# Weights loaded by row chunk, a list schedule with a lower rate for the first loads, and group 1's x transposed on TensorE

## The chip, the cores and the metric

The kernel runs on one core of one Trainium2 chip. The metric is the device time of that core in microseconds (us), the median of several executions. TensorE is called PE in the profile (PEld is its weight load), VectorE is DVE, ScalarE is ACT, GpSimd is POOL, and SP is the engine that issues the DMAs.

## What is computed

Four graph layers run over a batch of 128 graphs with 128 nodes and 512 features each. Every layer adds its result to x and normalizes:

```python
def _layernorm(x, axis=-1, eps=1e-5): ...
# layer 0
Ah = A + eye; dh = rsqrt(sum(Ah, -1)); An = dh[:, :, None] * Ah * dh[:, None, :]
x = _layernorm(x + relu(einsum('bnm,bmf,fc->bnc', An, x, kernel) + bias))
# layer 1
q, k = split(einsum('bnd,ed->bne', x, W_qk)); v = einsum('bnd,ed->bne', x, W_v)
w = softmax(sum((q @ k^T) / 8 * adj, -1), over the nodes)
x = _layernorm(x + w * v)
# layer 2
agg = einsum('bij,bjf->bif', adj, x) / maximum(deg, eps)
x = _layernorm(x + relu(einsum('bnf,of->bno', concat([x, agg]), W)))
# layer 3
L = A_hat * d[:, :, None] * d[:, None, :]            # A_hat = adj + eye
x = _layernorm(x + L @ (x @ W + b))
```

All data are float32. x is 32 MB and adj 8 MB; each of the five 512 x 512 weights (w0, wv, the two halves w2x and w2a of layer 2, and w3) is 1 MB.

## The kernel before

The batch is worked through in 32 groups of G = 4 graphs. A group's x is one tile of 128 partitions (the nodes) by 4 graphs by 512 features, its adjacency one of 128 by 4 by 128. An aggregation is a set of 128x128 matmuls that leave its result transposed (`aggregate`, into PSUM tiles p_agg, copied by ScalarE to agg). A product with a weight (`project`) is done in seven block products in place of eight: for each pair of graphs of a group, the left operand is cut into four blocks (two graphs by two feature halves), the weight into four 256 x 256 blocks, and sums of blocks are multiplied. The names of the seven are B11, T1, B21, B22, T2, T3 and T4. `weight_sums` makes T1 to T4 of a weight by four subtractions on 128x512 elements, `left_sums` the four sums of the left side (agg0s, xT1s, xT2s, agg2s, agg3s in the profile). The products go into PSUM regions named p_o (layers 0, 2 and 3) and p_v (layer 1); VectorE takes them out in steps (u_o, u_v, s_o). The product T4 and what follows it is put off as a "tail", which the next `project` runs after its own B11 (`finish_tails`). `hooks` put other work of TensorE after a named product.

Layer 1 needs x transposed, and there are two ways to do it. `turn_x` writes x to a scratch tensor in DRAM, reads it back in another order (2 + 4 DMAs per half group, xT1s and xT1y) and has VectorE transpose 32 x 32 blocks. `turn_on_tensor` copies x on ScalarE into a tile y, transposes it by 4 matmuls per graph (p_xT) and copies the result back on ScalarE (xT). `l1_turn(t, turn, rows)` takes either.

`begin` (line 829) writes out the order of the first two groups by hand, the loop behind it that of the other 30, and the last lines (879 to 886) that of the last group, in which layers 2 and 3 run for a half group at a time.

The order of the instructions on TensorE is the program's. For all other engines it is set by `Plan.schedule` (line 195), a list schedule made while the kernel is built: `estimate` gives every operation a duration, each gets the latest time at which it must end for TensorE not to wait, and every engine takes of its ready operations the one that is due first. Once issued, each engine works strictly in this order. For DMAs, issued by SP alone, the schedule holds a model of the transfers: the line

```python
bus = max(bus, op.end + self.LAND) + op.size / self.BUS
```

says that they pass one behind another at BUS = 95 elements of 4 bytes per ns, and that the first byte takes LAND = 1600 ns. It also models that a VectorE operation with two operands in SBUF and a GpSimd operation exclude each other (`port`).

At the start the loads of group 0 and 1 go out, then the weights. `weight` loads each by its four blocks, so that a row of a piece is 256 elements (1 KB); wv and w2x come in a permuted row order (`turned`), with 16 DMAs each, the others with 4. The tile is `[P, 7, 2, H]`: block, chunk of 128 rows, column. Behind them come adj and x of groups 2 and 3. adj of group 2 is wanted by `prep_rows(2)`, which sums it (deg), takes the power -1/2 on GpSimd (d), and makes the scaled matrices ana.

All operations are issued from one helper, so nearly all rows of the profile have line 266 and are told apart by their tiles.

Of the kernel before, what the change touches and what calls it, by code (L numbers as in the profile page):

```python
# [10 lines left out]
FP = mybir.dt.float32  # L11
AF = mybir.ActivationFunctionType
ALU = mybir.AluOpType
AX = mybir.AxisListType

P = 128
K = 32
Q = P // K
# [3 lines left out]
H = F // 2  # L22
# [103 lines left out]
class Plan:  # L126
# [4 lines left out]

    ENGINES = ("tensor", "vector", "scalar", "gpsimd", "sync")
    HOP = 200
    LAND, BUS = 1600, 95

    def __init__(self, nc, est):
        self.nc, self.est, self.ops, self.tags, self.group, self.dram = nc, est, [], {}, None, None
# [57 lines left out]
    def schedule(self):  # L195
        number = {op: i for i, op in enumerate(self.ops)}
        for (_, tag, bufs), tiles in self.tags.items():
            used = []
            for t in sorted((t for t in tiles if t.ops), key=lambda t: number[t.ops[0]]):
                if len(used) == bufs:  # L200
                    old = used.pop(min(range(bufs), key=lambda i: number[used[i].ops[-1]]))
                    assert number[old.ops[-1]] < number[t.ops[0]], (tag, bufs)
                    for op in t.ops:
                        if op.preds.isdisjoint(t.ops):
                            op.preds.update(old.ops)
                used.append(t)
        now = 0
        for op in self.ops:
            assert all(number[p] < number[op] for p in op.preds)
            for p in op.preds:  # L210
                p.succs.append(op)
            if op.engine == "tensor":
                op.last = now
                now += op.dur
        for op in reversed(self.ops):
            due = min([s.last - self.hop(op, s) for s in op.succs], default=now)
            op.last = min(op.last, due - op.dur)
        queue = {e: [] for e in self.ENGINES}
        waiting = {op: len(op.preds) for op in self.ops}
        free, bus, port = dict.fromkeys(self.ENGINES, 0), 0, 0  # L220
        pe = [op for op in self.ops if op.engine == "tensor"]
        for op in self.ops:
            if not op.preds:
                queue[op.engine].append((0, number[op], op))
        done = []
        while len(done) < len(self.ops):
            best = None
            for e in self.ENGINES:
                q = queue[e]
                if e == "tensor":  # L230
                    q = [c for c in q if c[2] is pe[0]]
                if not q:
                    continue
                q = [(max(c[0], port if c[2].port else 0),) + c[1:] for c in q]
                at = max(free[e], min(c[0] for c in q))
                pick = min((c for c in q if c[0] <= at), key=lambda c: (c[2].last, c[1]))
                for c in q:
                    if at < c[0] < at + pick[2].dur and c[2].last < at + pick[2].dur and c[2].last < pick[2].last:
                        pick, at = c, c[0]
                if best is None or at < best[0]:  # L240
                    best = at, e, pick[2]
            at, e, op = best
            queue[e] = [c for c in queue[e] if c[2] is not op]
            op.start, op.end = at, at + op.dur
            free[e] = op.end
            if op.port:
                port = op.end
            if e == "sync":
                bus = max(bus, op.end + self.LAND) + op.size / self.BUS
                op.lat = max(op.lat, bus - op.end)  # L250
            if e == "tensor":
                pe.pop(0)
            done.append(op)
            for s in op.succs:
                waiting[s] -= 1
                if not waiting[s]:
                    queue[s.engine].append((max(p.end + self.hop(p, s) for p in s.preds), number[s], s))
        return done
# [48 lines left out]
def kernel(  # L307
# [16 lines left out]
    last = NT - 1  # L324
# [31 lines left out]
    def weight(src, name, queue, turned=False):  # L356


        w = const.tile([P, 7, 2, H], FP, tag=name, name=name)
        for h in range(2):  # L360
            for j in range(2):
                s = src[:, j * H:(j + 1) * H]
                if turned:
                    s = s.rearrange("(b h c k) m -> h b k c m", b=Q, h=2, c=2)[h]
                    for b in range(Q):
                        queue.dma_start(w[b * K:(b + 1) * K, 2 * h + j], s[b])
                else:
                    queue.dma_start(w[:, 2 * h + j], s.rearrange("(h c p) m -> h p c m", h=2, c=2)[h])
        return w

    def weight_sums(w, eng):
        eng.tensor_tensor(w[:, T3], w[:, B22], w[:, T1], ALU.subtract)
        eng.tensor_tensor(w[:, T1], w[:, T1], w[:, B11], ALU.subtract)
        eng.tensor_tensor(w[:, T2], w[:, B22], w[:, T1], ALU.subtract)
        eng.tensor_tensor(w[:, T4], w[:, B21], w[:, T2], ALU.subtract)

    def broadcast_row(src, name, queue):
        r = const.tile([P, F], FP, tag=name, name=name)
# [136 lines left out]
    def project(name, t, parts, first, c11, fin, hooks=None, after=lambda: None, early=True,  # L515
                when=lambda f: f(), pairs=(0, 1)):

        hooks = hooks or {}  # L520
        qs = slice(pairs[0], pairs[-1] + 1)

        def region():
            return ps_b.tile([P, 2, H], FP, tag="pb", name=f"p_{name}_{t}")[:, qs]

        def operand(left_, k):
            s = st[left_, t]
            if isinstance(s, Ref):
                return s.rearrange("p (q r) (h c) n -> p q r h c n", r=2, h=2)[:, :, 0, (B11, B21).index(k)]
            return s[k]  # L530

        def product(p, k, fresh):
            with nc.unit():
                for q in pairs:
                    for i, (left_, w) in enumerate(parts):
                        for c in range(2):
                            nc.tensor.matmul(p[:, q - pairs[0], :], operand(left_, k)[:, q, c, :], w[:, k, c, :],
                                             start=(fresh and q == pairs[0] and i == 0 and c == 0),
                                             stop=(i == len(parts) - 1 and c == 1), skip_group_check=True)
            for f in hooks.get(k, ()):  # L540
                f()

        def block(tag):
            return tp.tile([P, 2, H], FP, tag=tag, name=f"{tag}_{name}_{t}", bufs=1 if tag in ("u5", "sb") else 2)[:, qs]

        g, q, v = region(), None, None
        product(g, B11, True)
        sa, sb = first(g, block)
        finish_tails()
        if early:  # L550
            product(g, B21, False)
            when(lambda: c11(g, block))
        q = region()
        product(q, T1, True)
        u5 = block("u5")
        nc.vector.tensor_tensor(u5, q, sb, ALU.add)
        if not early:
            product(g, B21, False)
            when(lambda: c11(g, block))
        v = region()  # L560
        product(v, T2, True)
        u2 = block("u2")
        nc.vector.tensor_tensor(u2, v, sb, ALU.add)
        product(q, B22, False)
        nc.vector.tensor_tensor(u2, q, u2, ALU.add)
        when(lambda: (fin(0, 1, u2), norm_stats(name, t, 0, pairs)))
        product(v, T3, False)
        nc.vector.tensor_tensor(u5, v, u5, ALU.add)
        fin(1, 1, u5)

        def tail():
            product(v, T4, False)
            nc.vector.tensor_tensor(sa, v, sa, ALU.add)
            fin(1, 0, sa)
            norm_stats(name, t, 1, pairs)
            after()

        tails.append(tail)
# [56 lines left out]
    def l0_agg(t, eng=nc.gpsimd, pairs=(slice(0, 2),)):  # L635
        left("agg0", t)
        for g in range(G):
            aggregate("agg0", t, g, st["anT", t])
        left_sums("agg0", t, eng, pairs)
# [189 lines left out]
    def begin():  # L829
# [3 lines left out]
        weight_sums(w0_sb, nc.gpsimd)  # L833
        l0_agg(0, nc.vector, ONE_BY_ONE)
        prep_rows(1)
        l0_out(0, {B11: [lambda: prep_transpose(1)], B22: [lambda: l0_agg(1)]})
        weight_sums(wv_sb, nc.vector)
        l0_out(1)
        l1_turn(0, turn_on_tensor, (0,))
# [3 lines left out]
        l1_qk(0, 1)  # L843
        for w in (w2x_sb, w2a_sb, w3_sb):
            weight_sums(w, nc.gpsimd)
        l1_turn(1)
        l1_out(0, {B11: [lambda: l1_scores(0)], B21: [lambda: l1_softmax(0)], T3: []})
        finish_tails()
        for r in range(2):
            l1_qk(1, r)  # L850
        l2_both(0, 0)

    def prep(t):
# [23 lines left out]
            l2_agg(t, 0)  # L877

    l2_both(last, 0)
    for q in range(2):  # L880
        l2_out(last, {B21: [lambda: l2_both(last, 1)]} if q == 0 else {}, (q,))
    for q in range(2):
        l3_agg_pair(last, q, nc.gpsimd)
        l3_bias(last, (2 * q, 2 * q + 1))
# [34 lines left out]
```

## Time and profile before

| | |
|---|---|
| runs (us) | 2486.29, 2488.41, 2488.83; median 2488.41 |
| span of the profiled execution | 2486.8 us, mean granted clock 0.997 |
| DMA, core queue | 398624 packets, 240.98 MB, 36.2% of 16 engines |
| SP, first 50 us | 8 loads of adj, x; 44 of the five weights; 4 of W_qk; 2 of biases |
| PE busy, 236 to 312 us (one group) | 76.00 of 76.00 us |
| PE busy, 0 to 100 us | 82.2 of 100 us |
| PE busy, last 27 us | 16.9 of 27 us |

The page's second part cuts the span into 40 slices; its row for PE is 8, then nines, then 8 again, so a group in the middle keeps TensorE busy throughout, and the times at which it is idle lie in the first and last few groups. A chain of waits at these places is read from the timeline: each row has the start, the time spent, engine, operation, tiles, and in brackets the idle time before it with what ended it. The column after the busy times in a table of stretches is the clock that TensorE was granted.

### The profile page before, as it was taken

The numbers are of one execution on the slowest core, as the hardware profiler recorded it, in microseconds if no ns is written. First come the engines' busy times: TensorE is split into PE (matmuls) and PEld (weight loads), VectorE is DVE, ScalarE is ACT, GpSimd is POOL, SyncE is SP. The second block draws the span as 40 slices with busy tenths as digits, with TensorE's granted clock in tenths as the row PEclk, the third lists the DMA queues.
The fourth block names the chain that finished last, engine by engine and source line by source line (L and its number), as shares of the span: only waits on it lengthen the run. The fifth ranks groups of instructions, "written<-read, shape, count | busy, mean of one in ns | idle before, by whom it ended". The sixth has DMA issues, their size and how long they took to land.

```text
span 2486.8 us, 37083 instructions
## 1 busy us (share of the span) xinstructions
PE 2457.3 (99%) x13470; PEld 2206.9 (89%) x13470; DVE 1810.0 (73%) x3169; ACT 973.2 (39%) x1981; POOL 1334.0 (54%) x1522
## 2 busy tenths in 40 slices
PE   8899999999999999999999999999999999999998
PEld 7789988989999899899899998998898999989987
DVE  6677777777777777777777777777777777777665
ACT  2334434343344343343433443433434434443335
POOL 5446555555556464555555564645555555645443
PEclk9999999999999999999999999999999999999999
DMA  5333434333344324343243443343442434423220
GB/s 178 69 93 81 108 88 123 111 78 101 98 106 123 94 77 109 91 124 110 72 107 93 112 123 88 79 111 93 123 110 68 112 90 115 118 81 86 77 60 34
DMA packets 398805, 243.34 MB, mean 98 GB/s; under 512 B 140832, under 2 KB 365600, under 8 KB 398624
## 3 DMA queue, kind: packets, MB, share of 16 engines
q1 hardware_dynamic: 398624, 240.98, 36.2%
q8 instruction: 107, 1.75, 0.3%
q14 instruction: 74, 0.61, 0.1%
HBM read 127.66 MB, written 113.25 MB: 97 GB/s over the span
## 4 chain that ended last, share of the span: by engine, by line
PE 97%; SPq 1%; DVE 1%; DMA 1%; ACT 0%; issue 0%; POOL 0%; ACTq 0%; POOLq 0%; DVEq 0%
PE p_o L266 61%; PE p_v L266 16%; PE p_agg L266 14%; PE p_qk L266 5%; PE p_sc L266 1%; SPq L266 1%; DMA x<-in_x_dram 0%; DVE x L266 0%; PE p_ws L266 0%; ACT xT L266 0%; PE p_w L266 0%; DMA adj<-in_adj_dram 0%; PE p_xT L266 0%; ACT agg L266 0%; DVE wv_sb L266 0%
## 5 line engine op out<-in xcount | busy, mean ns | idle before, releaser
L266 ACT COPY agg<-p_agg 128x512 f32<-128x512 f32 x384 | 221.3, 584 | 573.1 <-PE p_agg L266 573.1
L266 PE MATMUL p_o<-w_sb,agg 128*128 128x256 f32 x1536 | 353.4, 379 | 0.5 <-DVE u_o L266 0.5
L266 PEld LDWEIGHTS p_o<-w_sb,agg 128*128 128x128 f32 x1536 | 286.7, 190 | 37.3 <-DVE u_o L266 0.9
L266 PE MATMUL p_o<-w2x_sb,xT2s 128*128 128x256 f32 x1024 | 263.0, 379 | 3.1 <-DVE xT2s L266 3.1
L266 PE MATMUL p_o<-w2a_sb,agg2s 128*128 128x256 f32 x1024 | 262.8, 379 | 0.0
L266 POOL TENSOR_TENSOR xT1s<-xT 128x512 f32<-128x512 f32 x64 | 94.1, 1471 | 290.2 <-DVE xT L266 220.1
L266 PE MATMUL p_agg<-anT,x 128*128 128x128 f32 x2048 | 243.9, 277 | 0.3 <-DVE anT L266 0.3
L266 PE MATMUL p_o<-w_sb,agg0s 128*128 128x256 f32 x1024 | 230.0, 383 | 7.0 <-DVE u_o L266 5.9
L266 PEld LDWEIGHTS p_agg<-anT,x 128*128 128x128 f32 x2048 | 235.4, 192 | 1.3 <-DVE anT L266 0.6
L266 PE MATMUL p_v<-wv_sb,xT1s 128*128 128x256 f32 x1024 | 233.3, 381 | 0.0
L266 POOL TENSOR_TENSOR agg3s<-agg 128x512 f32<-128x512 f32 x62 | 84.1, 1357 | 272.3 <-ACT agg L266 272.3
L266 PEld LDWEIGHTS p_o<-w_sb,agg0s 128*128 128x128 f32 x1024 | 193.5, 192 | 34.2 <-POOL mro L266 4.9
L266 PEld LDWEIGHTS p_o<-w2x_sb,xT2s 128*128 128x128 f32 x1024 | 194.4, 190 | 29.9 <-DVE xT2s L266 3.6
L266 PE MATMUL p_o<-w_sb,agg3s 128*128 128x256 f32 x992 | 219.2, 379 | 0.0
L266 PEld LDWEIGHTS p_o<-w2a_sb,agg2s 128*128 128x128 f32 x1024 | 194.6, 190 | 26.5
L266 PEld LDWEIGHTS p_v<-wv_sb,xT1s 128*128 128x128 f32 x1024 | 189.6, 190 | 27.3
L266 PEld LDWEIGHTS p_o<-w_sb,agg3s 128*128 128x128 f32 x992 | 188.5, 190 | 25.6
L266 ACT ACTIVATE x<-x,nmro,rstdo 128x512 f32<-128x512 f32 x257 | 198.7, 809 | 4.8 <-ACT nmro L266 0.3
L266 PE MATMUL p_o<-w2x_sb,xT 128*128 128x256 f32 x768 | 197.5, 380 | 1.2 <-ACT s_o L266 0.7
L266 PE MATMUL p_o<-w2a_sb,agg 128*128 128x256 f32 x768 | 197.1, 379 | 0.0
L266 DVE TENSOR_TENSOR u_o<-p_o,s_o 128x512 f32<-128x512 f32 (+1 forms) x132 | 89.2, 675 | 145.3 <-PE p_o L266 145.3
L266 PE MATMUL p_v<-wv_sb,xT 128*128 128x256 f32 x768 | 181.6, 379 | 0.9 <-DVE u_v L266 0.9
(141 smaller groups left out, 4662.1 us busy)
## 6 DMA issues: line engine op xcount, KB each, us to landing
x<-in_x_dram SPq DMA_DIRECT2D x31, 1024.0 KB, 5.1
xT1s<-x SPq DMA_DIRECT2D x124, 256.0 KB, 2.5
xT1y<-xT1s SPq DMA_DIRECT2D x248, 128.0 KB, 3.3
out_dram<-x SPq DMA_DIRECT2D x31, 1024.0 KB, 5.4
xT2s<-x SPq DMA_DIRECT2D x120, 256.0 KB, 2.6
xT2y<-xT2s SPq DMA_DIRECT2D x240, 128.0 KB, 2.8
sa<-ana SPq DMA_DIRECT2D x120, 128.0 KB, 3.3
ya<-sa SPq DMA_DIRECT2D x120, 128.0 KB, 3.2
```

What stands on the lines that cost most here:

```text
L266: getattr(getattr(self.nc, op.engine), method)(*[v.real() if isinstance(v, Ref) else v for v in args], **{k: v.real() if isinstance(v, Ref ...
```

## The change

The weights get tiles `[P, 2, 7, H]`: chunk first, then block. A load brings both column blocks of a row half at once, so that a row of a piece is 512 elements (2 KB). The plain weights take 2 DMAs and the turned ones 8; the sums and the products address the tile by chunk.

The schedule's transfer model takes 62 elements per ns for DMAs issued up to 40 us of the plan and 95 after that, and lets an issue of SP wait until no more than nine DMAs are on their way (this for the whole plan).

In `begin`, the transposes of group 1's adjacency come after the product B21 of group 0's layer 0 instead of after B11. Group 1's x for layer 1 is transposed by `turn_on_tensor`, after the product T3 of group 0's layer 1 (behind the transpose p_ws of its softmax weights), followed by the first half of its p_qk; before, it was turned by `turn_x` ahead of that layer, and both halves of p_qk came after the tail. At the end, the tail of group 30's layer 3 is taken out of the list before layer 2 of the last group, and runs after `l2_both(last, 1)` rather than ahead of it.

```diff
-    LAND, BUS = 1600, 95
+    LAND, FLIGHT = 1600, 9
+    HEAD, BUS = 40000, (62, 95)
...
+            if e == "sync" and len(landed) >= self.FLIGHT:
+                at = max(at, landed[-self.FLIGHT])
             op.start, op.end = at, at + op.dur
...
-                bus = max(bus, op.end + self.LAND) + op.size / self.BUS
+                bus = max(bus, op.end + self.LAND) + op.size / self.BUS[at > self.HEAD]
                 op.lat = max(op.lat, bus - op.end)
+                landed.append(op.end + op.lat)
...
-        w = const.tile([P, 7, 2, H], FP, tag=name, name=name)
+        w = const.tile([P, 2, 7, H], FP, tag=name, name=name)
         for h in range(2):
-            for j in range(2):
-                s = src[:, j * H:(j + 1) * H]
-                if turned:
-                    s = s.rearrange("(b h c k) m -> h b k c m", b=Q, h=2, c=2)[h]
-                    for b in range(Q):
-                        queue.dma_start(w[b * K:(b + 1) * K, 2 * h + j], s[b])
-                else:
-                    queue.dma_start(w[:, 2 * h + j], s.rearrange("(h c p) m -> h p c m", h=2, c=2)[h])
+            to = w[:, :, 2 * h:2 * h + 2].rearrange("p c j m -> p c (j m)")
+            if turned:
+                for b in range(Q):
+                    queue.dma_start(to[b * K:(b + 1) * K], src.rearrange("(b h c k) m -> h b k c m", b=Q, h=2, c=2)[h][b])
+            else:
+                queue.dma_start(to, src.rearrange("(h c p) m -> h p c m", h=2, c=2)[h])
...
-        eng.tensor_tensor(w[:, T3], w[:, B22], w[:, T1], ALU.subtract)
+        eng.tensor_tensor(w[:, :, T3], w[:, :, B22], w[:, :, T1], ALU.subtract)
...
-                            nc.tensor.matmul(p[:, q - pairs[0], :], operand(left_, k)[:, q, c, :], w[:, k, c, :],
+                            nc.tensor.matmul(p[:, q - pairs[0], :], operand(left_, k)[:, q, c, :], w[:, c, k, :],
...
-        l0_out(0, {B11: [lambda: prep_transpose(1)], B22: [lambda: l0_agg(1)]})
+        l0_out(0, {B21: [lambda: prep_transpose(1)], B22: [lambda: l0_agg(1)]})
...
-        l1_turn(1)
-        l1_out(0, {B11: [lambda: l1_scores(0)], B21: [lambda: l1_softmax(0)], T3: []})
+        l1_out(0, {B11: [lambda: l1_scores(0)], B21: [lambda: l1_softmax(0)],
+                   T3: [lambda: l1_turn(1, turn_on_tensor), lambda: l1_qk(1, 0)]})
         finish_tails()
-        for r in range(2):
-            l1_qk(1, r)
+        l1_qk(1, 1)
         l2_both(0, 0)
...
     l2_both(last, 0)
+    held = tails.pop()
     for q in range(2):
-        l2_out(last, {B21: [lambda: l2_both(last, 1)]} if q == 0 else {}, (q,))
+        l2_out(last, {B21: [lambda: l2_both(last, 1), held]} if q == 0 else {}, (q,))
```

## The prediction

> **What bounds the kernel now.** I read the page first, then the waits of TensorE by stage, then its timeline and that of the engine it waits for, and last the stretches with their granted clock.
>
> ```profile
> span 2486.8 us, 37083 instructions
> PE 2457.3 (99%) x13470; PEld 2206.9 (89%) x13470; DVE 1810.0 (73%) x3169; ACT 973.2 (39%) x1981; POOL 1334.0 (54%) x1522
> ```
>
> TensorE is busy for all but 2486.8 - 2457.3 = 29.5 us. The waits of TensorE between 160 and 2380 us are an empty list, so a change of order and of loads can gain only at the two ends. The waits of TensorE from 0 to 160 us (total, times, longest), of which I show the ones that the change touches:
>
> ```profile
> PE p_o L266 <- DVE u_o L266: 5.9, 2, 4.5
> PE p_qk L266 <- DVE xT L266: 3.9, 1, 3.9
> PE p_a L266 <- DVE ana L266: 1.6, 1, 1.6
> ...
> PE p_o L266 <- POOL agg0s L266: 1.0, 1, 1.0
> PE p_v L266 <- DVE u_v L266: 0.9, 1, 0.9
> ```
>
> The timeline of TensorE puts the two long ones at 40.84 to 45.37 us and at 73.77 to 77.66 us. Their price is more than their length, as two stretches show (PE busy, PEld, DVE, ACT, POOL, then the granted clock):
>
> ```profile
> 45.40:51.70 6.30, 6.30 (x18) 5.07 (x19) 2.50 (x6) 2.58 (x5) 5.41 (x7) 0.58 0.04 14
> 77.70:83.10 5.40, 5.40 (x34) 5.40 (x35) 5.40 (x7) 2.75 (x5) 5.13 (x6) 0.68 0.01 3
> ```
>
> Behind each long wait the clock is 0.58 and 0.68. 16 matmuls of 128x256 take 6.32 us there and 3.46 us (16 at 0.2165) in the long rows elsewhere, 2.86 us more; the 32 of p_qk take 5.44 us instead of 2 x 1.78, 1.88 us more. Why the first wait is there, VectorE's timeline says:
>
> ```profile
> 30.93 0.69 DVE L266 TENSOR_TENSOR u_o<-p_o,u_o 128x512 f32<-128x512 f32 x1 [1.87 <-PE p_o L266]
> 35.92 0.69 DVE L266 TENSOR_REDUCE deg<-adj 128x4 f32<-128x512 f32 x1 [4.29 <-DMA adj<-in_adj_dram]
> ...
> 44.55 0.68 DVE L266 TENSOR_TENSOR u_o<-p_o,sb_o 128x512 f32<-128x512 f32 x1
> ```
>
> VectorE stands 4.29 us for adj_2, with the eviction u_o for which TensorE will wait queued behind. adj_2 is issued by SP only at 33.02 us. Between 16.5 and 33 us the DMA moves 2.85 MB at 172 GB/s, against 322 GB/s from 6 to 16 us: there the queue is short of issues. 33 pieces, mostly 64 KB, leave SP at 0.43 us each plus 0.04.
>
> At the end (2380 us on), the page's chain is TensorE until 2438, with one wait inside that the change touches:
>
> ```profile
> PE p_o L266 <- DVE xT2s L266: 1.6, 1, 1.6
> ```
>
> **What the Trainium skill says.** "TensorE: Matmul & The Clock Gate", What's actually happening: an idle window of about 3.4 us puts the array back to half rate, until it has been busy as long. The trace agrees: the 4.53 and 3.88 us waits are followed by 0.58 and 0.68, those of 1.6 us and less by 1.00. "SBUF — State Buffer", Who interferes with whom: a VectorE operation with two inputs in SBUF and a GpSimd operation that reads SBUF exclude each other for a whole instruction. Here the wv_sb subtraction takes 0.69 to 1.76 us, the long ones while GpSimd is busy. "DMA: Bandwidth & Descriptors", Specifications: rows from 512 B on reach line rate. The weights' rows have 1 KB before and 2 KB after, so longer rows alone should give little; the 322 GB/s stretch, mostly packets under 2 KB, agrees.
>
> **The change, part by part.**
>
> Larger pieces. w0, w2a and w3 go from 4 DMAs to 2, wv and w2x from 16 to 8: 22 issues fewer on SP, at 0.47 us some 10 us. In the starved stretch 33 become about 17, 8 us instead of 16.5; the same 2.85 MB at 322 GB/s take 8.9 us. So adj_2 lands about 7.5 us earlier, near 28.5 us instead of 35.9. GpSimd's w2a sum, which stood 11.31 us for its load until 32.11, comes earlier too and no longer sits late before agg0s. The first product needs a 512 KB piece where 256 KB served; all of w0 has landed by 11.43 us before (GpSimd starts its sum then) and the product starts at 12.14: no cost. The strided operands of the 20 subtractions keep 128x512 elements: 0, as the strided xT1s take 1.27 us like the weights.
>
> The plan. Its rate for issues up to 40 us falls from 380 to 248 GB/s (62 elements of 4 B per ns), with at most nine loads in flight. In the plan adj and weights land later than before, so VectorE and GpSimd put other work ahead. Two consequences: d of group 1 (1.01 us on GpSimd, at 12.65 behind the first w0 sum) can go first, at about 10 us, and deg of group 2 leaves its place ahead of u_o. Nine in flight holds for the whole plan; later landings make it careful, not the chip slower.
>
> B11 to B21. The product B21 (8 x 0.2165 = 1.73 us) runs where TensorE stood 1.56 us for ana, and the transposes follow. But VectorE, 13.70 to 25.63 without a pause and stretched by GpSimd, then sets T1, T2 and B22 (waits of 0.16 and 1.34). With d earlier it starts its run about 1.6 us sooner. I take 1.6; bounds 0 (the later waits take it all) and 3.1 (all three go).
>
> The wait for agg0s (1.01): GpSimd starts agg0s at 35.77 behind w2x, although agg is complete at 29.79. With the load early I take 1.0; bounds 0 and 1.0.
>
> The wait for u_o. Without the 4.29 us stand, and with the run before it about 1.6 earlier, VectorE reaches u_o near 44.55 - 4.29 - 1.6 = 38.7; TensorE comes to it at 40.84 - 1.6 - 1.0 = 38.2. Eviction 0.7 and start add up to a wait of about 1.0 in place of 4.53, too short for the slow clock: 3.5 + 2.86 = 6.4. Bounds 1.5 (3 us of wait with a slow clock) and 7.4.
>
> Group 1's x on TensorE. Out go 12 DMAs (2.71 + 4.22 us on SP) and 4 stream transposes (2.49 us of VectorE), and with them the wait of 3.88, its slow clock of 1.88, and the 0.85 for u_v, under which the transposes now lie: 6.6. In come 16 transposes on TensorE (8 take 0.89): 1.8; 4 copies of 0.56 and 4 of 0.59 on ScalarE, which is idle from 66.6 to 78.2 (11.64 us), behind which nothing on the path queues. New: TensorE reaches p_agg of group 0 about 7.3 us after p_ws instead of 12.2. x needs 0.2 for ws, 0.7 for u_v, 1.9 for 4 updates, 1.6 for statistics, 1.3 on GpSimd, 1.0 on ScalarE, 6.8 in all; GpSimd holds two updates up by 2.0 now, and its four xT1s sums may do so. I take a wait of 1.0, net 6.6 - 1.8 - 1.0 = 3.8; bounds 1.5 and 4.8.
>
> The held tail. The 8 matmuls of the last T4 of group 30 (1.73) move from before l2_both(last, 1) into the wait of 1.58 behind it. VectorE's two operations on it (0.69 each) have nothing on the path behind them if they follow xT2s; ScalarE's norm of that group moves some us later, under the products up to 2458. I take 1.4; bounds 0 and 1.6.
>
> Sum: 1.6 + 1.0 + 6.4 + 3.8 + 1.4 = 14.2 us. The profiled execution took 2488.74 by the clock of the other runs, its span being 2486.8; the three runs shown have 2486.29 to 2488.83. 2488.41 - 14.2 = 2474.2. The bounds sum to 3.0 and 17.9.
>
> **Rivals.** (1) VectorE and GpSimd bound the start. From 10 to 50 us they are busy for 28.4 and 24.5 us, and they exclude each other. Then each wait taken out returns at the next eviction, and about half is left: 7, 2481.4. For it: 1.34 follows 1.56 so closely. Against it: 4.29 and 11.31 us of their idle time are waits for loads. (2) The change does little at the start: loads land as before, because bandwidth bounds them, or the plan keeps its order. Then group 1's turn and the tail give 3.8 + 1.4, less what shifts: about 4, 2484.4. Against it: 172 GB/s. (3) Slower: in the steady groups the new plan puts a VectorE operation that waits for a load ahead of an eviction. At 1219.04 a stream transpose stands 0.48 us for its DMA already, at 1246.68 2.16, and B22 starts at 1224.64, only 0.8 us after the T1 eviction ends. Some 29 groups repeat it: 14.2 / 29 = 0.5 us each eats the gain, beyond 0.7 it is slower by more than 0.2%; at 1 us, 2474.2 + 29 = 2503. Against it: SP is idle most of a group, so nine in flight seldom binds, and it makes landings later in the plan, not earlier.
>
> **How the numbers follow.** Forecast 0.72, rival 1 0.13, rival 2 0.08, rival 3 0.07. A measurement of this kernel tells about 0.2%, 5 us, from no change, which ends at 2483.4. Faster: the forecast, rival 1, and 0.03 of rival 2 = 0.88; within: 0.05 of rival 2; slower: rival 3. The range runs from 2470 (the upper bounds nearly all) to 2482.5 (rival 1 with a us to spare), leaving rivals 2 and 3 out.
>
> **What would show it.** In the changed profile: no wait of TensorE over 2 us in the first 100 us, no clock under 0.9 from 10 us on but at the very end; adj_2 landing before 30 us; deg without a wait on DMA ahead of u_o; p_qk of group 1 behind p_xT at once; no xT2s wait at the end; and still an empty list from 160 to 2380 us. A wait list there, a p_agg wait over 3 us at 68 us, or a long wait in the 30s would make it wrong.

## The result and the profile after

The changed kernel takes 2480.97 us (median of 6 runs, 2479.61 to 2481.86) against 2487.88 for the kernel before in the same comparison: 6.9 us less, ratio 0.9972, 95% interval [0.9959, 0.9984]. It is faster, by about half of the 14.2 us that were forecast. The page's head:

```profile
span 2479.5 us, 37052 instructions
PE 2458.4 (99%) x13486; PEld 2206.8 (89%) x13486; DVE 1813.6 (73%) x3165; ACT 976.6 (39%) x1989; POOL 1336.5 (54%) x1522
```

The span is 7.3 us shorter, and TensorE's busy time has hardly moved. The waits of TensorE from 0 to 160 us, as before (total, times, longest):

```profile
PE p_o L270 <- DVE u_o L270: 2.6, 1, 2.6
PE p_v L270 <- DVE u_v L270: 1.9, 1, 1.9
PE p_o L270 <- DVE xT2s L270: 1.5, 1, 1.5
PE p_o L270 <- ACT s_o L270: 1.3, 2, 0.7
...
PE p_o L270 <- DVE agg0s L270: 0.8, 3, 0.4
```

The waits of 4.53 us (u_o), 3.88 (xT), 1.56 (ana) and 1.01 (agg0s) are gone. Two have grown in their place: a wait for u_o of 2.61, which was 1.34, and one for u_v of 1.95, which was 0.85. Their places on TensorE's timeline, and how long the instructions behind them took:

```profile
23.60 1.99 PE L266 MATMUL p_o<-w_sb,agg0s 128*128 128x256 f32 x8 [1.34 <-DVE u_o L266]
...
71.78 1.99 PE L266 MATMUL p_v<-wv_sb,xT 128*128 128x256 f32 x8 [0.85 <-DVE u_v L266]
```

So it was before. In the changed kernel:

```profile
25.10 3.64 PE L270 MATMUL p_o<-w_sb,agg0s 128*128 128x256 f32 x8 [2.61 <-DVE u_o L270]
...
39.06 7.35 PE L270 MATMUL p_o<-w_sb,agg0s 128*128 128x256 f32 x32
...
71.41 2.42 PE L270 MATMUL p_v<-wv_sb,xT 128*128 128x256 f32 x8 [1.95 <-DVE u_v L270]
73.62 3.21 PE L270 MATMUL p_qk<-wqk_sb,xT 128*128 128x128 f32 x16
```

The first product behind the wait of 2.61 takes 3.64 us, where before it took 1.99; behind 1.95, 16 of p_qk take 3.21 where 1.95 to 2.04 is usual. The 32 matmuls at 39.06 run through: there the kernel before stood 4.53 us. The stretches show the slow clock (the column after POOL):

```profile
20.00:30.00 10.00, 7.13 (x29) 5.61 (x30) 7.43 (x13) 0.33 (x1) 2.18 (x2) 0.83 1.05 275
70.00:80.00 10.00, 8.21 (x48) 7.50 (x48) 7.57 (x16) 5.00 (x12) 7.04 (x10) 0.83 0.01 3
```

What VectorE does ahead of both evictions, its timeline says:

```profile
23.10 0.75 DVE L270 TENSOR_TENSOR agg0s<-agg 128x256 f32<-128x256 f32 x2
23.76 0.68 DVE L270 SCALAR_TENSOR_TENSOR x<-u_o,x 128x512 f32<-128x512 f32 x1
24.37 1.28 DVE L270 TENSOR_TENSOR u_o<-p_o,sb_o 128x512 f32<-128x512 f32 x2
...
37.05 0.67 DVE L270 TENSOR_REDUCE deg<-adj 128x4 f32<-128x512 f32 x1
...
66.69 2.68 DVE L270 SCALAR_TENSOR_TENSOR x<-u_v,ws,x 128x256 f32<-128x256 f32 x2
69.29 1.27 DVE L270 BATCH_NORM_STATS2 bnv<-x 128x6 f32<-128x512 f32 x2
...
70.69 0.66 DVE L270 TENSOR_TENSOR u_v<-p_v,u_v 128x512 f32<-128x512 f32 x1
```

VectorE is not idle ahead of u_o at 24.37 or u_v at 70.69. It does work for which nothing on TensorE is waiting: two sums for T3 and an update of x; then updates of x and statistics. The sum of adj_2 (deg, 37.05) no longer waits for its load. From 160 to 2380 us the list of TensorE's waits is still empty.

With TensorE's milestones the 7.3 us fall into the prediction's terms (start of the operation, us). The steps are those of one profiled execution of each kernel; the spans of the changed kernel's six executions lie between 2477.8 and 2480.1 us.

| milestone | before | after | step gains | predicted |
|---|---|---|---|---|
| l0_agg of group 1 (B11 to B21) | 25.43 | 28.58 | -3.15 | +1.6 |
| T1 of group 1 (agg0s) | 37.09 | 39.06 | +1.18 | +1.0 |
| p_ws (the u_o wait) | 70.71 | 65.44 | +7.24 | +6.4 |
| first p_agg of layer 2 (group 1's x) | 82.94 | 76.67 | +1.00 | +3.8 |
| l0_agg of group 2 | 112.25 | 106.21 | -0.23 | 0 |
| the end (held tail), spans | 2486.8 | 2479.5 | +1.26 | +1.4 |

### The profile page after: what moved, and what is told of

Same layout as the page of the kernel before. It is cut to its first block, busy times and chain, and to the rows that moved or that the text cites. A ratio compares the mean times of both kernels' runs of the same rounds, so it can differ in the third digit from the quotient of the medians.

```text
span 2479.5 us, 37052 instructions
## 1 busy us (share of the span) xinstructions
PE 2458.4 (99%) x13486; PEld 2206.8 (89%) x13486; DVE 1813.6 (73%) x3165; ACT 976.6 (39%) x1989; POOL 1336.5 (54%) x1522
## 3 DMA queue, kind: packets, MB, share of 16 engines
q8 instruction: 107, 1.75, 0.3%
## 4 chain that ended last, share of the span: by engine, by line
PE 98%; DMA 1%; ACT 0%; DVE 0%; SPq 0%; POOL 0%; issue 0%; ACTq 0%; POOLq 0%; DVEq 0%
PE p_o L270 62%; PE p_v L270 16%; PE p_agg L270 14%; PE p_qk L270 5%; PE p_sc L270 1%; DMA x<-in_x_dram 0%; SPq L270 0%; DVE x L270 0%; PE p_ws L270 0%; DMA w2x_sb<-in_L_gnn_W_dram 0%; PE p_w L270 0%; ACT xT L270 0%; PE p_xT L270 0%; POOL last L270 0%; ACT agg L270 0%
```

## The experiments

Times are medians, each with the kernel before on the same chip; spans are those of the profiled executions. "Ratio" is to the kernel before.

**e1, the change without the new plan.**

```diff
-    LAND, FLIGHT = 1600, 9
-    HEAD, BUS = 40000, (62, 95)
+    LAND, BUS = 1600, 95
```

> The changed kernel with the schedule's transfer model of before (95 elements per ns throughout, no limit in flight); pieces, order and tail stay. Theory: the lower rate makes VectorE do the last left sums and an x update before the eviction u_o that B22 of group 0 waits for, so without it B22 starts by 23.6 us instead of 25.1 and its clock stays full; the time falls by about 3, to 2478. Rival: the plan is what keeps the sum of adj_2 out of VectorE's way; without it the wait of 4.5 us ahead of group 1's B22 comes back, and the time rises by 3 to 6, to 2484 or more.

Measured: 2491.15 against 2488.06, ratio 1.0012 [1.0006, 1.0019], span 2489.2. The other parts without the plan are slower than no change. The theory held as far as B22 of group 0, which starts at 22.66 us with its clock full. Then the rival's wait comes back: the load of adj_2 comes earlier, but its sum stands in front of the evictions again (VectorE idle 6.33 us until 31.71), and TensorE stands for the eviction behind it:

```profile
38.53 5.54 PE L266 MATMUL p_o<-w_sb,agg 128*128 128x256 f32 x16 [6.86 <-DVE u_o L266]
```

A wait of 3.1 us in three pieces, for rs, also appears in the steady groups. On the whole the rival was right: the earlier load does not take the wait out without the plan's place for the sum.

**e2, the transposes of group 1 behind B11 again.**

```diff
-        l0_out(0, {B21: [lambda: prep_transpose(1)], B22: [lambda: l0_agg(1)]})
+        l0_out(0, {B11: [lambda: prep_transpose(1)], B22: [lambda: l0_agg(1)]})
```

> The changed kernel with the adjacency transposes of group 1 behind B11 again. Theory: VectorE's left sums bound T1 and T2 there, whatever TensorE does between; B22 of group 0 starts at 25.1 us as in the changed kernel, the time is 2481 within 0.5. Rival: the move of B21 itself costs what was lost before B22; then B22 starts near 23.6 and the time falls by 3, to 2478. The prediction's value for the move, a gain of 1.6, would make it 2482.6.

Measured: 2478.76, ratio 0.9966 [0.9952, 0.998], span 2478.9. l0_agg of group 1 starts at 26.92, 1.66 us earlier than in the change, although the u_o wait is 3.68; some of the slow clock then falls into l0_agg itself, and at the next product (31.23 against 32.15) 0.92 is left. By the whole time this is not told from the change. The move B11 to B21 brought nothing here and may have cost a us. One way in which it costs is SP's order. In this run adj_1 is issued ahead of the first piece of w0, and its sum starts at 8.89 us:

```profile
2.27 0.47 SPq L270 DMA_DIRECT2D adj<-in_adj_dram  x1
...
8.89 0.69 DVE L270 TENSOR_REDUCE deg<-adj 128x4 f32<-128x512 f32 x1 [0.70 <-DMA adj<-in_adj_dram]
```

In the change the first piece of w0 goes at 2.27 and adj_1 at 2.78, and the sum starts at 9.86. All runs with the move have this order, also e1 without the plan and e5 with small pieces, and none without the move has it.

**e3, group 1's x through DRAM again.**

```diff
-        l1_out(0, {B11: [lambda: l1_scores(0)], B21: [lambda: l1_softmax(0)],
-                   T3: [lambda: l1_turn(1, turn_on_tensor), lambda: l1_qk(1, 0)]})
+        l1_turn(1)
+        l1_out(0, {B11: [lambda: l1_scores(0)], B21: [lambda: l1_softmax(0)], T3: []})
```

(and both halves of p_qk after the tail)

> The changed kernel with group 1's x turned through DRAM, ahead of layer 1 of group 0, and both p_qk behind the tail. Theory: the turn on TensorE brought only about 1 us, since a wait of 1.95 us and a slow clock came in its place; the time rises by 1, to 2482, with a wait of some 4 us of p_qk on VectorE's xT. Rival, the prediction: it brought 3.8; the time is 2484.8.

Measured: 2482.13, ratio 0.9975 [0.9966, 0.9985], span 2480.4: 0.9 us more in span, 1.2 in median. The wait for xT is back (2.51, with 5.44 us for the 32 matmuls behind it). By the whole time the two are not told apart; by the milestones of the profiles the turn was worth about 1 us, and the 2484.8 of the rival lies above all of the ten executions (2483.87 at most).

**e4, the kernel before with the larger pieces alone** (the diff's part in `weight`, `weight_sums` and `project`).

> The kernel before with nothing but the weights in larger pieces. Theory: the 5.3 us won between 37 and 51 us come from the earlier landing of adj_2 and of w2; the wait of 4.53 us for u_o shrinks under 1.5 us and its slow clock goes; gain 5 to 7, time 2482. Rival: the gain there comes from the plan's later landing times, which take the sum of adj_2 out of VectorE's way; then the pieces alone gain under 2, time 2486 to 2488.

Measured: 2487.92, ratio 1.0001 [0.9992, 1.0009]. No gain. SP issues adj_2 at 25.99 us instead of 33.02, as predicted, but VectorE gets it only at 32.11:

```profile
32.11 0.69 DVE L266 TENSOR_REDUCE deg<-adj 128x4 f32<-128x512 f32 x1 [9.28 <-DMA adj<-in_adj_dram]
```

From issue to use it takes 6.1 us, before 2.9. The loads ahead of it are still under way: the DMA moves 275 GB/s from 26.0 to 32.1 us, against 218 from 33.0 to 35.9 before. And VectorE, with the sum still ahead of u_o, now stands 9.28 us for it instead of 4.29, and TensorE 7.42 us for u_o instead of 4.53.

**e5, the change with the small pieces of before** (the same part undone).

> The changed kernel with the weights in the small pieces of before; plan, order and tail stay. Theory: the plan alone puts the sum of adj_2 late enough on VectorE (37.05 us in the changed kernel, after even the landing of before, 35.9), so the small pieces cost at most 1, by GpSimd's w2 sum standing ahead of agg0s; 2481 to 2482. Rival, the prediction: the earlier landing is what takes the waits away; then a wait of several us for u_o comes back ahead of group 1's B22, and the time is 2485 or more.

Measured: 2480.86, ratio 0.997 [0.9959, 0.9981]; the change has 2480.97. With the plan too the pieces bring nothing that can be measured.

**e8, the kernel before with the new plan alone** (only the diff's lines in `Plan`).

> The kernel before with the new plan alone (62 elements per ns for the first loads, nine in flight); small pieces, old order of begin, old tail. Theory (the plan is what brings the gain at the start, the pieces nothing): 2482, 5 to 6 us below before: the u_o wait of 4.53 us and its slow clock are gone, the wait for xT (3.9) and the xT2s wait at the end (1.6) are still there. Rival (the plan needs the larger pieces or the new order to work, as in the kernel without plan the parts without it cost 3 us): within 1.5 us of before, 2486.5 or more, with VectorE again standing 4 us or more for adj_2 ahead of u_o. Second rival (the plan is worth in any company the 10.2 us that separate the change from the change without plan): 2478.

Measured: 2480.42, ratio 0.9966 [0.9953, 0.998], span 2478.5: 8.3 us below the span before. The median is 7.4 us lower, more than the 5 to 6 of my theory, which lie within the interval, and less than the 10.2 of the second rival, which lie within it too. The plan alone gives a gain that is not told from that of the whole change. TensorE's timeline at the places in question:

```profile
23.81 2.77 PE L270 MATMUL p_o<-w_sb,agg0s 128*128 128x256 f32 x8 [2.61 <-DVE u_o L270]
...
37.78 7.07 PE L270 MATMUL p_o<-w_sb,agg0s 128*128 128x256 f32 x32
...
69.47 5.33 PE L270 MATMUL p_qk<-wqk_sb,xT 128*128 128x128 f32 x32 [2.44 <-DVE xT L270]
...
103.95 3.73 PE L270 MATMUL p_agg<-anT,x 128*128 128x128 f32 x32
```

And VectorE's sum of adj_2:

```profile
42.04 0.68 DVE L270 TENSOR_REDUCE deg<-adj 128x4 f32<-128x512 f32 x1
```

adj_2 is issued here at 33.89 us and takes 2.9 to land, so it comes a little later than before (33.02 and 2.9), and the wait is gone all the same: its sum stands behind the evictions and waits for nothing. The 32 matmuls behind 37.78 run through, and the wait of 2.61 for u_o is already here: the plan's new order makes it, with B11 as with B21. l0_agg of group 2 (103.95) even starts 2.3 us before that of the change; the tail at the end, where the wait of 1.57 for xT2s is still there, takes 1.3 of it back.

**e6, the evictions first.** The change, with the third left sums and the first update of x moved behind u_o of T1, and u_v of T4 moved ahead of the updates of x and the statistics.

```diff
+        first = find("u5_o0_0")[0]
+        late = [op for op in find("agg0s3_0") + find("x_0", "u2_o0_0")[:1] if done.index(op) < done.index(first)]
+        done = [op for op in done if op not in late]
+        i = done.index(first) + 1
+        done[i:i] = late
+        v = find("u5_v_0")[1]
+        done.remove(v)
+        i = done.index(find("ws_0")[0]) + 1
+        done[i:i] = [v]
```

> The changed kernel, all operations the same, with three of VectorE's moved behind an eviction: the third left sums and the first x update of group 0 behind u_o of T1, and the x updates and statistics of layer 1 behind u_v of T3. Theory: their places are what TensorE's waits of 2.61 and 1.95 us come from; B22 of group 0 starts 1.3 us earlier (23.8), T4 of layer 1 right behind p_qk (69.5 in the changed kernel's times), and a slow clock follows neither; the sum is 1.3 + 1.9 + 1.95 + 1.8, less up to 2 for x of group 0 coming later, so 5 to 7: 2475. Rival: VectorE's and GpSimd's sum of work bounds these stretches; the waits come back at T2, T3 or p_agg of group 0, and the time falls by under 2.

Measured: 2478.72, ratio 0.9967 [0.9954, 0.998], span 2476.2, 3.3 below the change. Both waits and their slow clock shrank as the theory said (the u_o wait to 1.33 and no longer slow behind it, the u_v wait gone), and the first product of layer 2 starts at 75.29, 4.7 us earlier than in the change (80.01). But the wait for xT2s grows from 1.50 to 2.56, and at 89.00 us only 3.3 of the 4.7 are left (after: 92.29). The 5 to 7 us of the theory did not come about: 3.3 in the span, 2.25 in the median.

**e7, the waits filled.** The change, with 10 matmuls between T2 and B22 and 8 between p_qk and T4 whose results nobody reads, so that the clock stays up though the waits remain.

```diff
+    def fill(n):
+        p = ps_t.tile([P, C, P], FP, tag="pt", name="p_fill")
+        with nc.unit():
+            for _ in range(n):
+                nc.tensor.matmul(p[:, 0], ident, ident, start=True, stop=True)
```

> The changed kernel with matmuls that nobody reads in its two waits: 10 of 128x128 (20 passes, 2.2 us) between T2 and B22 of group 0, and 8 (1.8 us) between group 1's first p_qk and T4. VectorE's order is the changed kernel's. Theory: the half clock behind these waits, 1.9 us and 1.8 us of longer matmuls, comes from idle time of TensorE; with it filled the clock stays 1.0 at 25 to 29 us and at 71 to 76 us, and the time falls by 3 to 3.7, to 2477.5. Rival: the half clock has another cause, or the fill delays B22 and T4 as much as it speeds what follows; no change within 1.

Measured: 2482.39, ratio 0.9977 [0.9967, 0.9986], span 2481.7. Three stretches:

```profile
22.00:30.00 8.00, 7.51 (x53) 7.01 (x54) 7.04 (x15) 0.92 (x2) 0.35 (x1) 1.00 1.10 241
68.00:76.00 8.00, 7.86 (x63) 7.43 (x61) 7.36 (x15) 3.84 (x9) 5.54 (x6) 1.00 0.01 2
88.00:96.00 8.00, 4.34 (x10) 3.54 (x11) 6.67 (x11) 0.73 (x2) 0.00 (x0) 0.66 0.00 0
```

The clock is 1.00 in both filled places, and layer 2 starts at 77.17, 2.8 us early. So the theory holds for the clock, and fails for the time: the third stretch takes the gain back, with a wait of 3.66 for xT2s and a clock of 0.66. VectorE has the reason:

```profile
85.20 0.69 DVE L270 TENSOR_REDUCE deg<-adj 128x4 f32<-128x512 f32 x1 [7.77 <-DMA adj<-in_adj_dram]
...
87.77 0.71 DVE L270 STREAM_TRANSPOSE anT<-ya 128x512 f32<-128x512 f32 x1 [1.40 <-DMA ya<-sa]
...
90.92 0.68 DVE L270 TENSOR_TENSOR xT2s<-xT 128x512 f32<-128x512 f32 x1
```

Ahead of the xT2s sums VectorE stands for the load of adj_3 and for group 2's transposes, which come at the DMAs' time; a TensorE that is earlier only waits longer. In the change deg stands 7.02 us there too.

**e9, e10: that last wait taken away as well.** e9 is e6, e10 is e7, with the sum of adj_3, its small operations and group 2's two stream transposes put behind the last agg2s sum of group 0.

```diff
+        late = [op for n in ("deg_3", "dh_3", "dm_3", "rdeg_3", "anT_2", "arT_2") for op in find(n)]
+        stop = done.index(find("agg2s3_0")[-1])
+        for op in done[:stop]:
+            if op not in late and not op.preds.isdisjoint(late):
+                late.append(op)
+        late = [op for op in done[:stop] if op in late]
+        done[stop + 1:stop + 1] = late
+        done = [op for i, op in enumerate(done) if i > stop or op not in late]
```

> The changed kernel with the evictions first (as in the run of that name) and, on VectorE, the sum of adj_3 with its three small operations and the two stream transposes of group 2 put behind the last agg2s sum of group 0. Theory (what took back a part of the gain were VectorE's operations that stand for DMAs ahead of the first agg2s and xT2s sums): TensorE's wait for xT2s falls from 2.56 to about 1.6, what agg, xT and the sums need after p_xT; span about 1.0 below the run with evictions first, near 2475.2, median about 2477.7. Rival (ScalarE's copies of agg and xT set that wait, or the moved operations come late for l0_agg of group 2): wait for xT2s unchanged or a new wait of 1 us or more for anT between 98 and 110 us, 2478.7 or more.

> The changed kernel with the waits at 22 and 70 us filled by the 18 matmuls that nobody reads, as in the run with filled waits, and VectorE's operations on adj_3 and on group 2's transposes put behind the last agg2s sum of group 0. Theory (the filled waits brought 2.8 us, and the wait of 3.66 us for xT2s with its slow clock at 88 to 96 us, set by the DMAs for which VectorE stood, took them back): wait for xT2s 1.8 or less, granted clock 0.95 or more from 84 to 100 us, span 2477 to 2478, 4 us below the run with filled waits (2481.7), and 1.5 to 2.5 below the change. Rival (the slow clock at 88 us has another reason, or the gain is lost again later): clock under 0.9 there again, or another wait of 2 us, and no gain over the change, 2480.5 or more.

Measured: e9 2476.60, ratio 0.9953 [0.9941, 0.9966], span 2474.9. e10 2478.18, ratio 0.9961 [0.9949, 0.9974], span 2476.3, 5.4 below e7 (4.2 in the median). TensorE in e10, where e7 stood 3.66:

```profile
89.04 1.13 PE L282 MATMUL p_o<-w2x_sb,xT2s 128*128 128x256 f32 x4 [1.50 <-DVE xT2s L282]
```

VectorE in e10, with no wait for a DMA left there:

```profile
88.30 0.69 DVE L282 TENSOR_TENSOR xT2s<-xT 128x512 f32<-128x512 f32 x1 [0.28 <-ACT xT L282]
...
94.01 0.68 DVE L282 TENSOR_REDUCE deg<-adj 128x4 f32<-128x512 f32 x1
```

The theory holds in both: what ate the gains of e6 and e7 was VectorE's order at 78 to 90 us. The 1.50 that is left is ScalarE's copy of xT and the sum behind it.

**e11, e9 with the transposes behind B11** (the edit of e2 added).

> As e9, with group 1's transposes behind B11 again as in the kernel before: the candidate for a version better than both. Theory: the move of the transposes costs 0.9 at 32 us, of which about half is lost again at the later waits, so 0.5 below e9, about 2477.2, with its best span near 2474.5. Rival (with the evictions first, the move brings what it was thought to bring, 1.6, since the later waits no longer take it): 1 to 1.6 us above e9.

Measured: 2476.30, ratio 0.995 [0.9938, 0.9963], span 2474.9, the same as e9. The 1.6 for B11 to B21 is not there with the evictions first either: at l0_agg of group 1 e9 is 0.50 ahead (25.60 against 26.10), at p_ws only 0.12 (63.11 against 63.23), and at l0_agg of group 2 0.06 behind. The rival, 1 to 1.6 us above e9, does not fit, as none of the five executions is above 2476.92; whether the move costs the 0.5 of the theory can't be told.

**e12, e11 with group 1's x through DRAM** (the edit of e3 added).

> The kernel of the run e11 (evictions first, the sum of adj_3 and the transposes of group 2 later, group 1's transposes behind B11) with group 1's x through DRAM as before, so the turn on TensorE is taken out where nothing eats its gain later. Theory (the turn is worth the wait for xT and its slow clock, which the run with the plan alone still has: 10.67 us from p_ws to the first p_agg of layer 2 against 7.85 in e11): 2.8 us later from there on, span 2477.7, median 2479. Rival (the turn brings about 1 as in the run without it, its cost on TensorE and ScalarE being as large as the wait): span 2476 or less, median 2477.3 or less.

Measured: 2475.64 against 2488.11, ratio 0.9951 [0.9938, 0.9965], span 2475.4. The rival is right: with VectorE's order mended the turn on TensorE brings nothing that can be told. The profiled spans differ by 0.5 us, the five of e12 among themselves by 2.4, and the median is not higher. TensorE in e12:

```profile
69.12 2.94 PE L291 MATMUL p_qk<-wqk_sb,xT 128*128 128x128 f32 x24 [1.71 <-DVE xT L291]
```

The wait for xT, 3.88 before, is 1.71 here with the same DMAs, of which SP starts the last eight 3.1 us earlier against p_ws, and no slow clock follows (24 in 2.94). In the kernel before, the four stream transposes start at 76.80, right behind the updates of x and the statistics from 71.64 on, without a wait for their DMA; in e12 one of the four is done at 62.45 and the updates take less. So that wait too looks like VectorE's queue more than the way through DRAM; no run moves the four transposes alone.

Together, in median us below the kernel before: pieces alone 0; plan alone 7.4; the whole change 6.9; the change without plan -3.1; plan, pieces and held tail with three places of VectorE's order mended (e12) 12.5. e9, e11 and e12 beat both kernels (every execution of theirs, 2477.62 at most, is below every one of the change, 2479.61 at least), and are not told apart from one another.

## Why the prediction was half right

Right: the change is faster, TensorE's 4.53 us wait for u_o and its slow clock go, deg of adj_2 no longer stands ahead of an eviction, the agg0s wait goes, the held tail is worth about what was said (1.26 for 1.4: the wait of 1.58 goes, one of 0.46 for s_o comes), and the steady groups keep an empty list, so rival 3 did not come about. Rival 1 (VectorE and GpSimd bound the start, about half is left: 7 us) is the case that came, and for much the reason it gave; it had 0.13. Three of the signs failed: a wait of 2.61 us where none over 2 was to be, a clock of 0.83 between 20 and 30 us and between 70 and 80, and adj_2, which lands at 31.4 us and not before 30.

Of the 6.9 us by which the span falls short of the forecast, term A below makes 4.75 and term D 2.80, while term C gave 0.84 more than was said. That the total fell on the 7 us of rival 1 is partly luck: that number was put down as about half, not worked out.

**Term A, B11 to B21: the step that failed.** "With d earlier it starts its run about 1.6 us sooner. I take 1.6; bounds 0 ... and 3.1." Measured -3.15, outside bounds that excluded a loss without a reason. d of group 1 does go first on GpSimd (10.83 instead of 12.65), but VectorE's sums agg0s start at 15.60 us, 0.23 later than before. The move itself puts adj_1 behind the first piece of w0 (e2), so deg of group 1 starts at 9.86 instead of 9.05. The product of adj and rdeg, done in 0.69 at 10.72 before, now comes behind that with d, beside GpSimd's sums, and takes 1.75; this comes with the plan alone too (e8, at 12.63). And 1.43 us of other work stand ahead of u_o. The eviction then comes too late for B22 (2.61 in place of 1.34), and 1.65 us of slow clock follow. In e2 and e8 part of the slow clock falls behind the start of l0_agg, so the shares are better read at the product behind it, which starts at 29.00 us before, 30.87 with the plan alone, 31.23 in the change without the move, and 32.15 in the change: 1.87 of the 3.15 come with the plan alone, and undoing the move gives 0.92 back. The prediction worked the move out as if the order of VectorE and of SP stood still around it.

**Term C: right in size, half wrong in mechanism.** "So adj_2 lands about 7.5 us earlier, near 28.5 us instead of 35.9." It is issued 7 us earlier and lands about 4 us earlier (e4), since with larger pieces it stays longer behind the loads ahead of it; rival 2 had said that. The earlier load alone gains 0 (e4), without the plan TensorE waits 6.86 us (e1), and with the plan alone the wait goes though adj_2 lands later than before (e8). It is the prediction's second reason, "deg of group 2 leaves its place ahead of u_o", that carries the 7.24 us.

**Term D: the size failed in one step.** "the 0.85 for u_v, under which the transposes now lie". The transposes lie there, but u_v does not come at its old time: with p_qk of group 1 ahead of T4, the plan lets VectorE do updates and statistics first, and the wait grows by 1.10 with 1.69 of slow clock behind it (2.42 and 3.21 us where 1.99 and 1.95 are usual). 3.88 + 1.88 - 1.10 - 1.69 - 1.83 (the transposes, 65.59 to 67.42) = 1.14; measured 1.00. The wait of p_agg for x, for which 1.0 was put down, did not come. In e12, with group 1's x still through DRAM, 1.71 and 0.85 are left of the 6.6 us that the turn was to take out, so some 4 of them needed no turn.

The pieces, of which the prediction made 10 us of SP's time, bring nothing measurable alone or with the plan. On the clock, the wait of "about 1.0 in place of 4.53, too short for the slow clock" did not come at all, and the limit I took from the Trainium skill did not hold: "TensorE: Matmul & The Clock Gate", What's actually happening, has about 3.4 us of idling ahead of the half rate. In these runs waits of 1.95 (after), 2.29 (e12), 2.41 (e11), 2.44 (e8) and 2.61 us (after, e8) were followed by slow matmuls, those of 1.71 and less were not, and one of 2.56 (e6) was not. Here the measurement decides: what limit holds, and what else enters it, stays open.

Shown by runs: the plan as the source of the gain (e1, e8), the worthless pieces (e4, e5), the clock behind the two waits (e7, e10), VectorE's order as what holds the rest back (e6, e9, e10). Also shown: that the move to B21 puts adj_1 behind w0 (e2). Only read from the traces: what that place cost by itself, and the value of the held tail, which no run has alone (the wait for xT2s at the end is in every run without it and in none with it). The plan has two parts, the lower rate and the limit of nine in flight; no run parts them, so which of them carries the gain is open. What the steady waits for rs in e1 come from was not tried either.

## What to carry to other kernels

When a list scheduler sets an engine's order, a wait named in the profile is often that order and not the transfer or the operation itself: look at what the engine did in the 3 us before the late eviction, and whether anyone was waiting for it. Changing a due time or a transfer rate can reorder everything near it, the loads too, so price the new order, not the moved instruction, and leave room below zero. A gain early in the program can be lost again at the next operation that comes at a DMA's time, as in e7; look for that pin before adding gains up.

## What the hardware showed that I had not expected

TensorE's clock fell after waits of 1.95 us and more, but for one of 2.56, as told above, and 10 and 8 matmuls of 128x128 that do nothing, put into two waits of 2.61 and 1.95 us, were enough to keep it at 1.00 there. A load issued 7.0 us earlier came only some 4 us earlier, 6.1 us after its issue in place of 2.9. And the same two sums of 128x256 on VectorE took 2.90 us at 15.60 and 0.75 at 23.10 in the changed kernel; GpSimd was busy with w0's sums in the first case, which agrees with "SBUF — State Buffer", Who interferes with whom, but the factor is larger than the stretching of 2.5 that I had reckoned with (0.69 to 1.76): each of the two sums takes 1.45, as long as one of GpSimd's operations there (1.45 at 16.76).
